# Two graph layers on one core: id transfers tied to a one-column copy, and one gathered bucket of seven in place of two

## The chip, the cores and the metric

The kernel runs on one core of one Trainium2 chip. The metric is the device time of one execution in microseconds (us), as the median of ten runs. A core has five engines that run their own instruction streams and wait for one another by semaphores: TensorE (PE, whose weight loads are shown apart as PEld), VectorE (DVE), ScalarE (ACT), GpSimd (POOL) and SyncE (SP). Plain transfers are issued here mostly from SP's queue; indirect transfers, which fetch rows by a list of row numbers, are issued from POOL's.

## What is computed

A graph has 6,250 nodes with 128 channels each and 200,000 edges (src, dst), sorted by dst. Two attention layers follow one another, each with a residual and a layer norm:

```python
# layer 0
hij = concat([h[src], h[dst]], -1)
exp_e = exp(leaky_relu(hij @ w, 0.2) @ a)
att = exp_e / segment_sum(exp_e, src)[src]
x = layernorm(x + segment_sum(h[src] * att, dst))

# layer 1: 4 heads of 32 channels
H = (x @ W) by head
s = exp(leaky_relu(Hs[src] + Ht[dst], 0.2) - max)
alpha = s / (segment_sum(s, src)[src] + 1e-8)
agg = segment_sum(alpha * H[dst], src) + x @ residual_projection
x = layernorm(x + elu(agg))
```

## The kernel before

Nodes are cut into 49 blocks of 128 (`NB`). An edge belongs to a bucket (i, j): i is the block of its source, j that of its destination. Each bucket has 128 slots, one edge per partition at most; `cols` holds, for each slot of each bucket, the row within the block of the edge's two ends, and -1 where the slot is empty. Seven buckets that follow one another are a chunk (`CH = 7`), so a row of 49 buckets has seven chunks. The instruction order on each engine is the order in which the program writes them.

**First stage (`score_edges`).** It loads the edges' ids, sorts them into slots, writes the table of slots to DRAM (`rows_jm`, `rows_im`) and computes the edge scores of layer 0. The ids of block j lie in a window of the sorted list; `find_windows` (L576) estimates where, and writes the row numbers of all windows into the tile `window_row`, one column for each block. `load_ids` (L599) then fetches the src and the dst ids of the next block with two indirect transfers on POOL, whose row numbers are column j of `window_row`. The tiles `ids0` and `ids1` hold a group of up to seven blocks and there are two of each, so a group's transfers wait until `split_ids` (L620) on DVE has read the group before last. `load_ids` is called at eleven fixed places of the prologue (`LOAD`, one block each) and later once for each row j, after its fourth chunk (L927). `split_ids` runs when the first block of a group is begun, three rows ahead of its scores. Nothing but the buffers and `window_row` holds the POOL queue back, so POOL issues whatever transfers have a tile free, far ahead of the place in the program. The work of this stage in `score_chunk` (L817) is six bf16 matmuls for each bucket on PE (L834), one operation for each bucket on DVE (L844), a one-hot over two rows of slots on DVE (L813), and transposes (L850).

**Layer 0's sum (from L1238).** For each destination block j, bucket by bucket, the weighted rows of the source nodes are needed, one per slot. There are two ways to get them. By PE: a one-hot of the slots (`OneHots`, L1123: SP fetches a row of slots spread to all partitions, DVE compares it, L1002) is multiplied with a table of the block split into three bf16 parts (`y3`), which takes three matmuls (`gather_b`, L1289); ACT copies the result out of PSUM (L1298). By DMA: an indirect transfer on POOL fetches 128 rows from the table `y_d` in DRAM (`Gathers`, L1073, the transfer at L1106). The constant `GP` says how many buckets of the seven are fetched by DMA, always the last ones of a chunk, and for rows r > 0 only (`by_dma`, L1069):

```python
    CUT = 3
    GP = 2
    BY_PE = CH - GP

    def by_dma(r, c):
        return r > 0 and c % CH >= BY_PE
```

A chunk is worked on in a group of three buckets and one of four (`groups_of_chunk`). For each bucket DVE also makes a weighted one-hot of the destinations (L1304), and one f32 matmul (two passes, two records in the trace) adds the bucket to the block's sum in PSUM (L1320). `scatter_loop` (L1049) puts the sums two groups behind the gathers. After each group, generators in `running` take one step: among them `nodes` (L1176), which runs once for each seven finished blocks and holds the layer norm, the products with layer 1's weights and the writing of `h_d` and `res_d` by SP (L1200, L1201). SP's queue also carries the fetches of the slots (L1142), in program order.

**Layer 1's sum (from L1337).** The same by source block i, with the table `h_d`, 132 columns wide (four heads of 32 channels and a one): `gather_c` (three bf16 matmuls for a bucket, L1419), `weigh_c` (a product with the attention weights on DVE, L1436, one operation for the buckets from PSUM and one for those gathered; a one-hot, L1443) and `sum_c` (L1457, f32, two records each). Between them stand the scores of the next row (L1367, L1368), whose one-hots of the sources are made by ACT (L997, L998) for all seven buckets. The one-hots of the destinations are made for all seven buckets too here, as the scores need them.

`Gathers.get` keeps five chunks of gathered rows ahead of their use, out of seven buffers. `Gathers.__init__` computes the row numbers of all gathered buckets on DVE (L1089), `GP` operations for each layer.

Of the kernel before, what the change touches and what calls it, by code (L numbers as in the profile page):

```python
# [11 lines left out]
I32 = mybir.dt.int32  # L12
# [4 lines left out]
P = 128  # L17
# [465 lines left out]
def score_edges(tc, keep, x, src, dst, w0, a0, rows_jm, rows_im):  # L483
# [4 lines left out]
    nc = tc.nc  # L488
# [26 lines left out]
    with ExitStack() as pools:  # L515
# [4 lines left out]
        fa = pools.enter_context(tc.tile_pool(name="fa", bufs=2))  # L520
# [41 lines left out]
        window_row = fc.tile([P, NB], I32, name="window_row")  # L562
# [36 lines left out]
        def load_ids():  # L599

            j = len(loaded_ids)
            if j == NB:
                return
            b = next(b for b, (c0, c1) in enumerate(id_groups) if c0 <= j < c1)
            c0, c1 = id_groups[b]
            if j == c0:
                ids[b] = [fi.tile([P, CH, WT], I32, name=f"ids{k}") for k in range(2)]
            for to, flat in zip(ids[b], (src, dst)):
                if j == NB - 1:
                    nc.sync.dma_start(to[:, j - c0, :], flat[E - WT * P :].rearrange("(p t) -> p t", t=WT))  # L610
                    continue
                nc.gpsimd.indirect_dma_start(  # L612
                    out=to[:, j - c0, :],
                    out_offset=None,
                    in_=flat[: NR * WT].rearrange("(r t) -> r t", t=WT),
                    in_offset=bass.IndirectOffsetOnAxis(ap=window_row[:, j : j + 1], axis=0),
                )
            loaded_ids.append(j)

# [244 lines left out]
        with tc.tile_pool(name="n0", bufs=3) as n0:  # L864
# [22 lines left out]
            for b in range(NB):  # L887
                if b % CH == 0 and b // CH + 2 < NC:
                    load_x(b // CH + 2)

                tp = pa[0].tile([P, 512], F32, name="u")[:, :P]
                nc.tensor.transpose(tp, xcs[b // CH][:, b % CH, :], ident)
                xt = n0.tile([P, P], F32, name="xt")
                nc.scalar.activation(xt, tp, AF.Copy)
                turned.append((b, xt))
                if b > 0:
                    tables(*turned.pop(0))
                if b == LOAD[0]:
                    find_windows(sampled)
                if b in LOAD:  # L900
                    load_ids()
                if b in BEGIN:
                    finding.append(find_slots(BEGIN.index(b)))
                    begun += 1
                if b >= BEGIN[0]:
                    find_more()
                if b == FIRST:
                    for k in range(3):
                        fetch(k)
                    one_hot(0)  # L910
                    one_hot(1)
                if b > FIRST and b % 4 == 0 and CH * (scored + 1) < b and scored + 1 < NC:
                    score_chunk(scored)
                    scored += 1
# [3 lines left out]
        for k in range(scored, len(order)):  # L918
            j, c = order[k]
            if c == 0 and j > 0:  # L920
                if j + AHEAD < NB:
                    finding.append(find_slots(j + AHEAD))
                elif j + 1 == NB:
                    finding.append(check_slots())
            score_chunk(k)
            find_more()
            if c == 3:  # L927
                load_ids()
# [6 lines left out]
def bucketed(ctx, tc, x, w1, al, ar, wr, out, cols, ex, den, rows_jm, rows_im):  # L935
    nc = tc.nc
# [122 lines left out]


    CUT = 3
    GP = 2
    BY_PE = CH - GP
    assert NB % CH == 0

# [7 lines left out]
    class Gathers:  # L1073


        def __init__(self, pool, table, which, ahead, width):
            self.pool, self.table, self.ahead, self.width = pool, table, ahead, width
            base_i = consts.tile([P, NC, GP], I32, name=f"base_i{which}")
            nc.gpsimd.iota(base_i, pattern=[[CH * P, NC], [P, GP]], base=BY_PE * P, channel_multiplier=0)
            base = consts.tile([P, NC, GP], F32, name=f"base{which}")  # L1080
            nc.vector.tensor_copy(base, base_i)

            self.ids = consts.tile([P, NB, NC, GP], I32, name=f"ids{which}")
            for q in range(GP):
                if which == 0:
# [536 lines left out]
@with_exitstack  # L1622
def kernel(ctx, tc, x, src, dst, w0, a0, w1, al, ar, wr, out):
    nc = tc.nc
    ctx.enter_context(tc.manual_schedule())
    NB = -(-x.shape[0] // P)
    keep = ctx.enter_context(tc.tile_pool(name="keep", bufs=1))
    dram = ctx.enter_context(tc.tile_pool(name="slots_d", bufs=1, space=bass.MemoryType.DRAM))
    rows_jm = dram.tile([NB, 2, NB, P], BF16, name="rows_jm")
    rows_im = dram.tile([NB, 2, NB, P], BF16, name="rows_im")  # L1630
    cols, ok, ex, den = score_edges(tc, keep, x, src, dst, w0, a0, rows_jm, rows_im)
    fits = nc.values_load(
        ok, min_val=0, max_val=1, skip_runtime_bounds_check_because="a product of two comparisons is 0 or 1"
    )
    with tc.If(fits == 1) as cmp:
        bucketed(tc, x, w1, al, ar, wr, out, cols, ex, den, rows_jm, rows_im)
    with cmp.Else():
        any_edges(tc, x, src, dst, w0, a0, w1, al, ar, wr, out)
# [35 lines left out]
```

## Time and profile before

| what | value |
|---|---|
| median of ten runs | 3640.07 us (3636.04 to 3643.8) |
| the profiled execution, its own time | 3636.17 us |
| its span, from the first to the last instruction | 3634.3 us |
| mean granted TensorE clock | 0.970 |
| PE busy | 3365.6 us (93% of the span) |
| DVE busy | 3177.8 us (87%) |
| ACT busy | 2027.2 us (56%) |
| POOL busy | 1496.1 us (41%) |
| indirect transfers of rows, layer 0 (`y_d`) | 672, mean 990 ns on POOL |
| indirect transfers of rows, layer 1 (`h_d`) | 672, mean 1065 ns on POOL |
| indirect transfers of ids | 96, mean 1122 ns (src) and 993 ns (dst) on POOL |

The profile is that of one execution. A row of it names an engine, a line of the code, the tiles it writes and reads, the number of instructions and the mean length of one. Lengths of instructions of one engine overlap where they are pipelined, so a group's busy time can be much less than number times mean; on PE that is the rule. The chain of waits follows the work that ended last back from the end, at each step to what released it; pieces of it on one engine add up without overlap, so they are the right place to read what one more instruction costs on that engine. The stages are, by their windows in the trace: prologue to about 90 us, first stage to 1518 us, layer 0's sum from about 1565 to 2510 us, layer 1's sum from about 2535 to 3560 us, and an end of some 70 us.

### The profile page before, as it was taken

Reading aid. Unit: us, or ns where it says so; the run is one execution under the profiler, and the core shown is the slowest. Engines: PE = TensorE matmul, PEld = TensorE weight load, DVE = VectorE, ACT = ScalarE, POOL = GpSimd, SP = SyncE. Lnnn points to the kernel's source line nnn. Section 1 sums busy time; section 2 is a strip of 40 time slices with the busy share of each in tenths; the row PEclk is TensorE's granted clock in tenths of the full one; section 3 lists DMA queues with packets and bytes.
Section 4 is the critical chain, followed back from the end, with each engine's and each line's share of the span. In section 5 each row is a group of like instructions: output and inputs, shape, how many; then the busy total and the mean of one; then the engine's idle time right before and its main releaser. Section 6 shows DMA issues by size and latency. Waiting matters only on the chain.

```text
span 3634.3 us, 125212 instructions
## 1 busy us (share of the span) xinstructions
PE 3365.6 (93%) x50166; PEld 3226.5 (89%) x50166; DVE 3177.8 (87%) x11723; ACT 2027.2 (56%) x3036; POOL 1496.1 (41%) x1474
## 2 busy tenths in 40 slices
PE   4699999999999999799999999997999999999996
PEld 3589989898989899788988988987999999999996
DVE  5688888888888888698888888888999999999997
ACT  4556666666666666343333333334666666666665
POOL 4001010101000000157766766764577676777771
PEclk7899999999999999899999999998999999999998
DMA  2133333343334433444444444445666676666662
GB/s 62 38 126 118 117 118 120 117 124 116 121 115 121 116 120 122 145 124 115 116 113 115 116 113 114 116 114 145 189 202 190 201 201 196 197 200 203 189 197 82
DMA packets 348224, 496.41 MB, mean 137 GB/s; under 512 B 65806, under 2 KB 325347, under 8 KB 347634
## 3 DMA queue, kind: packets, MB, share of 16 engines
q1 hardware_dynamic: 296520, 393.32, 36.0%
q0 software_dynamic: 46992, 94.52, 11.3%
q8 instruction: 399, 6.54, 0.7%
q14 instruction: 191, 1.56, 0.2%
q10 hardware_dynamic: 4122, 0.47, 0.1%
HBM read 472.71 MB, written 15.39 MB: 134 GB/s over the span
## 4 chain that ended last, share of the span: by engine, by line
PE 73%; DVE 16%; ACT 5%; issue 3%; DMA 3%; another core or an unknown queue 0%; POOL 0%; SPq 0%; ACTq 0%; DVEq 0%; POOLq 0%
PE u L1457 16%; PE oj L1320 14%; PE u L834 14%; PE he L1419 8%; PE ye L1289 7%; DVE junk L844 3%; PE tp L850 2%; PE sm L736 2%; DMA rows<-rows_jm 2%; DVE rows L813 2%; PE u L684 2%; PE sp L1368 2%; PE sm L673 1%; PE u L682 1%; DVE vst L711 1%
## 5 line engine op out<-in xcount | busy, mean ns | idle before, releaser
L834 PE MATMUL u<-pq,rows 128*128 128x130 bf16 x14406 | 914.9, 221 | 62.5 <-DVE junk L844 57.0
L834 PEld LDWEIGHTS <-rows 128*128 128x128 bf16 x14406 | 857.2, 98 | 76.3 <-issue 67.0
L1106 POOL DMA_INDIRECT rows_g<-h_d,ids x672 | 716.0, 1065 | 343.6 <-DVE z L1436 175.1
L1106 POOL DMA_INDIRECT rows_g<-y_d,ids x672 | 665.2, 990 | 293.7 <-PE oj L1320 151.3
L1304 DVE TENSOR_SCALAR oh<-iota_b,dsts,ex 128x128 f32<-128x128 bf16 x2401 | 668.8, 361 | 72.5 <-ACT dsts L1282 48.3
L1457 PE MATMUL u<-z,oh 128*128 128x132 f32 x4802 | 700.6, 286 | 0.0
L844 DVE SCALAR_TENSOR_TENSOR junk<-u,a_ext 128x130 bf16<-128x130 f32 x2401 | 547.6, 292 | 89.6 <-PE u L834 87.8
L1457 PEld LDWEIGHTS u<-z,oh 128*128 128x128 f32 x4802 | 592.1, 190 | 0.8
L852 ACT ACTIVATE oh<-tp 128x896 bf16<-128x896 bf16 x343 | 314.4, 917 | 451.5 <-PE tp L850 451.5
L1298 ACT ACTIVATE yc<-ye 128x384 f32<-128x384 f32 (+2 forms) x686 | 298.2, 438 | 478.1 <-PE ye L1289 462.3
L1320 PE MATMUL oj<-yc,oh 128*128 128x128 f32 x3458 | 542.5, 289 | 13.4 <-ACT yc L1298 11.0
L1320 PEld LDWEIGHTS oj<-yc,oh 128*128 128x128 f32 x3458 | 445.7, 194 | 17.1 <-ACT yc L1298 12.7
L1289 PE MATMUL ye<-y,rows 128*128 128x128 bf16 x5187 | 409.5, 222 | 51.7 <-DVE rows L1002 50.8
L1443 DVE TENSOR_TENSOR oh<-iota_b,cols 128x384 f32<-128x384 bf16 (+2 forms) x693 | 421.0, 608 | 0.0
L1419 PE MATMUL he<-h,rows 128*128 128x132 bf16 x5187 | 416.8, 221 | 0.0
L1289 PEld LDWEIGHTS <-rows 128*128 128x128 bf16 x5187 | 354.7, 100 | 69.7 <-DVE rows L1002 32.8
L612 POOL DMA_INDIRECT ids<-in_src_dram,window_row x48 | 53.9, 1122 | 763.8 <-DVE tmp L632 730.6
L1419 PEld LDWEIGHTS <-rows 128*128 128x128 bf16 x5187 | 358.2, 97 | 10.2
L1436 DVE TENSOR_TENSOR z<-he,w 128x396 f32<-128x396 f32 (+2 forms) x693 | 339.3, 490 | 24.5 <-PE he L1419 23.3
L997 ACT ACTIVATE rows<-rows,minus_p 128x896 bf16<-128x896 bf16 x336 | 346.2, 1030 | 23.4 <-DMA rows<-rows_im 13.2
L998 ACT ACTIVATE rows<-rows 128x896 bf16<-128x896 bf16 x336 | 319.3, 950 | 10.6
L1002 DVE TENSOR_SCALAR rows<-rows,part_f 128x896 bf16<-128x896 bf16 (+1 forms) x693 | 286.3, 414 | 6.6 <-DMA rows<-rows_im 3.2
(209 smaller groups left out, 4655.8 us busy)
## 6 DMA issues: line engine op xcount, KB each, us to landing
rows<-rows_jm SPq DMA_DIRECT2D x693, 224.0 KB
rows<-rows_im SPq DMA_DIRECT2D x686, 224.0 KB
rows<-rows_jm SPq DMA_DIRECT2D x336, 160.0 KB
rows_g<-y_d,ids POOLq DMA_INDIRECT x672
rows_g<-h_d,ids POOLq DMA_INDIRECT x672
h_d<-hx SPq DMA_DIRECT2D x6, 462.0 KB
xc<-in_x_dram SPq DMA_DIRECT2D x6, 448.0 KB
x_sb<-in_x_dram POOLq DMA_DIRECT2D x6, 448.0 KB
```

The costliest lines, as they stand in the source:

```text
L834: nc.tensor.matmul(u[:, d, :], rows[:, w, i - c0, :], pq3[:, b, w, s, :], start=(w == 0 and s == 0), stop=(w == 1 and s == 2),)
L844: nc.vector.scalar_tensor_tensor(junk, u[:, d, :], 0.0, a_ext, op0=OP.max, op1=OP.mult, accum_out=acc[:, i : i + 1])
L997: nc.scalar.activation(rows, rows, AF.Square, bias=minus_p)
L998: nc.scalar.activation(rows, rows, AF.Relu, bias=1.0, scale=-1.0)
L1106: nc.gpsimd.indirect_dma_start(out=t[:, q, :], out_offset=None, in_=self.table[:, :], in_offset=bass.IndirectOffsetOnAxis(ap=self.ids[:, r ...
L1289: nc.tensor.matmul(ye[:, k, :], oh[:, i0 + k - c0, :], y3[:, i0 + k, s, :], start=(s == 0), stop=(s == 2))
L1304: nc.vector.tensor_scalar(oh[:, k, :], iota_b, dsts[0][:, i : i + 1], ex[:, j, i : i + 1], op0=OP.is_equal, op1=OP.mult,)
L1320: nc.tensor.matmul(outs[j], oh[:, k, :], values[k], start=(i == 0), stop=(i == NB - 1))
L1419: nc.tensor.matmul(he[:, k, :], oh[:, j0 + k - c0, :], h3[:, j0 + k, s].rearrange("p h e -> p (h e)"), start=(s == 0), stop=(s == 2),)
L1436: nc.vector.tensor_tensor(z[:, a:b].rearrange("p n (h e) -> p n h e", h=H), rows.rearrange("p n (h e) -> p n h e", h=H), weights[i][:, j0 ...
L1443: nc.vector.tensor_tensor(oh[:, :n], iota_b[:, None, :].to_broadcast([P, n, P]), cols[:, j0 : j0 + n, 0, i : i + 1].to_broadcast([P, n, P] ...
L1457: nc.tensor.matmul(aggs[i], oh[:, k, :], z[:, k, :], start=(j == 0), stop=(j == NB - 1))
```

## The change

`load_ids` first copies column j of `window_row` into a small tile `row` of its own, on DVE, and the two transfers take their row numbers from that tile. The tile comes from the pool `fa`, which has two buffers for each name, so a copy also waits until the transfers of two blocks before have read theirs. For the last block, whose ids come by two plain transfers on SP, the copy is made but not used. And `GP` is 1 in place of 2, so `BY_PE` is 6: of each chunk of seven buckets, six come by PE and one by an indirect transfer, in both layers. The number of row numbers, the tiles of gathered rows (`[P, GP, width]`), the slots fetched for layer 0's one-hots (`needed`) and the parts of `weigh_b` and `weigh_c` follow from `GP`.

```diff
@@ load_ids
                 ids[b] = [fi.tile([P, CH, WT], I32, name=f"ids{k}") for k in range(2)]
+
+            row = fa.tile([P, 1], I32, name="row")
+            nc.vector.tensor_copy(row, window_row[:, j : j + 1])
             for to, flat in zip(ids[b], (src, dst)):
...
-                    in_offset=bass.IndirectOffsetOnAxis(ap=window_row[:, j : j + 1], axis=0),
+                    in_offset=bass.IndirectOffsetOnAxis(ap=row, axis=0),
@@ bucketed
     CUT = 3
-    GP = 2
+    GP = 1
     BY_PE = CH - GP
```

## The prediction

> **What bounds the kernel now.** I read the chain of waits first, by engine, and then the busy time of each engine by stage.
>
> ```profile
> PE 73%; DVE 16%; ACT 5%; issue 3%; DMA 3%; another core or an unknown queue 0%; POOL 0%; SPq 0%; ACTq 0%; DVEq 0%; POOLq 0%
> ```
>
> POOL, whose work the change halves, has no share of the chain. The stages (columns: window, length, busy us of PE, PEld, DVE, ACT, POOL with their instructions, granted clock, DMA share, GB/s):
>
> ```profile
> 90.00:1510.00 1420.00, 1327.60 (x24436) 1253.58 (x24435) 1208.05 (x5930) 885.00 (x1078) 58.84 (x54) 0.97 0.37 115
> 1600.00:2450.00 850.00, 807.38 (x9003) 788.33 (x9000) 740.09 (x2578) 319.14 (x819) 607.83 (x620) 0.99 0.47 115
> 2560.00:3580.00 1020.00, 1018.41 (x14501) 995.81 (x14500) 988.98 (x2438) 655.86 (x750) 702.00 (x658) 1.00 0.67 193
> ```
>
> Layer 0's sum (second line) leaves PE idle 42.6 us of 850, layer 1's (third) 1.6 of 1020. A busy PE could still hide waits, so I checked it against the chain, whose pieces do not overlap. One whole chunk of layer 0:
>
> ```profile
> 1917.65 0.50 PE ye L1289 x9
> 1918.15 0.72 PE oj L1320 x6
> 1918.87 0.34 PE ye L1289 x6
> 1919.21 0.95 PE oj L1320 x8
> ```
>
> These are nothing but matmuls end to end, 2.51 us: nine and six bf16 gathers (three buckets and two), and the sums of seven buckets. In row 0, where no bucket is gathered by DMA, the second group has four buckets by PE:
>
> ```profile
> 1571.56 0.67 PE ye L1289 x12
> 1572.23 0.95 PE oj L1320 x8
> ```
>
> 0.67 us for 12 against 0.34 for 6: each bf16 matmul takes 0.056 us of the chain, with gathers by DMA or without. In layer 1 the matching pieces are:
>
> ```profile
> 3003.04 0.35 PE he L1419 x6
> 3003.39 0.95 PE u L1457 x8
> 3004.35 0.52 PE he L1419 x9
> ```
>
> That is 0.058 us for each matmul (132 columns).
>
> **Part 1, GP from 2 to 1: what it adds on PE.** In each layer rows 1 to 48 have 7 chunks, so 336 buckets move to PE, three matmuls each: 1008 for a layer, with as many weight loads, which overlap (98% of PE's stretch in layer 1 shows PEld busy beside it). Layer 0: 1008 x 0.0556 (0.50 / 9) = 56.0 us. Layer 1: 1008 x 0.0584 (mean of 0.35 / 6 and 0.52 / 9, rounded up) = 58.9 us. PE sets the end in both, so both lie on the path: 114.9 us.
>
> **What it takes away.** 672 indirect transfers, about 1.03 us of POOL each, some 690 us of POOL. The waits of both windows say who waits for whom:
>
> ```profile
> POOL rows_g L1106 <- PE oj L1320: 114.0, 211, 5.5
> POOL rows_g L1106 <- DVE z L1436: 175.1, 225, 16.4
> ```
>
> POOL waits for the users of its buffers; of its 1344 gathers no engine but POOL itself is recorded as waiting for one (0.9 us). The gain is therefore nothing. If the five chunks that it fetches ahead were not cover enough, this could be worth something; the third rival prices that.
>
> **What moves on the other engines.** ACT copies 384 columns in place of 256 in layer 0 (490 against 382 ns): 336 x 0.108 = 36 us on an engine busy 319 of 850, one group ahead of its use; nothing. DVE's one-hot there covers 768 slots; the rows on each side are 381 ns (640) and 446 ns (896), so +0 to +65 ns, by position +32 ns, 11 us over the layer on an engine with 110 us free; nothing in the steady chunk. In layer 1 the weighing is 561 + 284 ns where it was 420 + 418: +7 ns a chunk, 2 us. DVE is 97% busy there, but PE's chunk grows by 0.175 us from 2.98, so DVE's share falls; without that cover it would cost 2 us. SP fetches 192 KB in place of 160 for a chunk of layer 0, while POOL's two gathers of 64 KB become one: 256 KB in place of 288. L1089 runs once in place of twice for each layer (753 ns): in layer 0's start it is in the chain, -1 us.
>
> **What gives some of it back.** Layer 0 stops PE after every seventh row, where `nodes` puts its steps on DVE and its two writes ahead of the next slots on SP's queue (the rows of slots issued behind them land after 6.7 us). Over the layer:
>
> ```profile
> PE ye L1289 <- DVE rows L1002: 24.3, 12, 2.7
> ```
>
> Two such stops per seven rows, 1.2 to 1.4 and 2.73 us, and one of 2.7 us at the layer norm (PE busy 7.34 of 10 us from 1825). They begin when PE has used up the two chunks of one-hots made ahead. Each chunk now lasts 0.167 us longer, so each stop shrinks by about 0.33 us: 3 x 0.33 x 6 = 6 us. The bounds: none (the larger rows land later by as much) to 20 us, as a shorter stop may keep the clock up too. After the 2.73 us stop the granted clock falls:
>
> ```profile
> 1717.00:1721.00 4.00, 1.27 (x13) 1.09 (x12) 2.53 (x9) 1.99 (x5) 1.94 (x2) 0.78 0.19 58
> 1721.00:1726.00 5.00, 5.00 (x34) 4.88 (x33) 5.00 (x18) 0.88 (x2) 0.17 (x1) 0.50 0.20 44
> ```
>
> Five us at half rate cost 2.5 us, up to 15 us over six stops. I take 6, from the stops alone: 2.4 us is nearer to 2.73, which lost the clock, than to 1.4, which did not. In layer 1 I take 1 us back, of PE's 1.6 us idle.
>
> [...]
>
> **Part 2, the copy.** 49 copies of one column on DVE. No row shows this one; the nearest are 141 ns for an operation on one column (L1408) and 191 ns for a copy of 98 columns (L746). So 49 x 0.1 to 0.19, 5 to 9 us of DVE, and 37 of the 49 lie in the first stage's rows. There the copy follows the fourth chunk, just ahead of the one-hot L813; in the row from 528 us that place is followed by DVE waiting 0.40 and 0.31 us for PE's L834, and the chain there is on PE. The copy is hidden by that wait; without it 37 x 0.14 = 5 us. Queued behind it on DVE stand L813 and the L844 that PE's PSUM buffers wait for. The copy waits for transfers issued two rows (55 us) before: no wait. POOL now issues two transfers per row and not 14 in a burst. Seven rows with a burst take 198.3 us (x24 pieces of L834 at 273.57, 471.87, 670.24), without one 197.8 (1066.00 to 1263.82); in a burst the splits L632 stretch from 0.28 to 0.49 us. Four bursts in the loop: -2 to -3 us. In the prologue POOL ran from 21.8 to 77 us without a pause; now the last ids of the second group are issued one block (about 3 us) ahead of the split that reads them. Two gathers at 1.25 us and a landing of at most 2.25 us (last issue 24.18, first split 26.43) make 4.75 us, so 0 to 2 us of wait for DVE. For the part: between -3 and +9 us, taken as -2 + 0 + 0.
>
> [...]
>
> **Sum.** 56.0 - 6 + 58.9 - 1 - 1 - 2 = 104.9 us on top of the profiled 3636.17 us: 3741. That execution lies 3.9 us under the median of 3640.07, so for a median the forecast is 3745 us. Its own range: -14 (half of the clock's 15 us too, and 6 in the first stage) to +11 (copies uncovered, stops unchanged): 3731 to 3756.
>
> **Rivals.** (a) *The stops in layer 0 mostly vanish.* For: they arise from DVE work and a late transfer, both measured against PE's pace, and each drags the clock. Against: 0.33 us of cover against stops of 1.4 and 2.7. Price: 42.6 us idle and 15 of clock; two thirds gone are 38 us in place of 6: 3713. (b) *Pacing turns into a wait.* For: in the prologue DVE has in-order work behind a copy that waits for two transfers to land. Against: the 2.25 us landing. Price: three waits of 2 us, 37 copies at 0.19 uncovered, no burst gain: 6 + 7 + 2 = 15: 3760. (c) *The gathers set PE's pace and its records only hide it*, so that halving them pays. For: two gathers take 2 x (0.94 + 0.30) = 2.5 us of POOL, almost the chunk's 2.51. Against: the same 0.056 us a matmul in row 0 without gathers, and POOL's waits. It decides if PE's own work in a chunk is under 2.51 - 0.17 = 2.34 us; at 2.2 us the layers would lose 0.14 x 672 = 94 us: 3546; at the point itself no change. (d) *The copy paces nothing*, as POOL would be as late anyway: -2 becomes 0, 3747, within the forecast.
>
> **How the numbers follow.** Forecast with (d) 0.78, (a) 0.09, (b) 0.11, (c) 0.02. The time is the forecast's, 3745. The range 3724 to 3760 takes in the half of (a) nearest to it and most of (b). A measurement tells 0.2% (7 us) from no change; only (c) is not slower by that: faster 0.02, same 0.01, slower 0.97.
>
> **What would show it.** Right: the chunk's chain in layer 0 reads 0.50, 0.72, 0.50, 0.95; layer 0's and layer 1's sums each last 50 to 59 us longer; 672 row gathers in all; seven rows of the first stage at 197.8 us or less throughout. Wrong: L1289 at other than 5187 + 1008 = 6195 matmuls, a DVE wait at the copy, or PE idle in layer 0 well under 35 us or over 45.

## The result, and the profile after

| | before | after |
|---|---|---|
| median | 3639.78 us (28 runs) | 3740.50 us (8 runs, 3737.01 to 3741.57) |
| profiled execution, its span | 3636.17, 3634.3 us | 3741.09, 3739.3 us |
| mean granted clock | 0.970 | 0.974 |

The ratio is 1.0274 with a 95% interval of [1.0265, 1.0283]: slower by 2.7%, or 100.7 us between the medians (96.5 to 103.0 by the interval). The forecast was 3745 us.

Where the 105.0 us between the two spans lie can be read from the first and the last matmul of each stage (us):

| | to the first score | first stage | gap | layer 0 | gap | layer 1 | end |
|---|---|---|---|---|---|---|---|
| before | 87.0 | 1429.5 | 25.3 | 969.1 | 23.5 | 1042.2 | 57.7 |
| after | 89.2 | 1430.4 | 25.0 | 1015.4 | 24.3 | 1094.8 | 60.2 |
| difference | +2.2 | +0.9 | -0.3 | +46.3 | +0.8 | +52.6 | +2.5 |

So the two layers' sums took nearly all of it. The shares of the chain of waits after:

```profile
PE 75%; DVE 15%; ACT 5%; issue 3%; DMA 2%; another core or an unknown queue 0%; POOL 0%; SPq 0%; ACTq 0%; POOLq 0%; DVEq 0%
```

PE's share rose by two points and POOL still has none. Windows of layer 0 and layer 1 as before (window, length, busy us of PE, PEld, DVE, ACT, POOL with their instructions, granted clock, DMA share, GB/s):

```profile
1600.00:2450.00 850.00, 814.08 (x9421) 796.33 (x9421) 706.41 (x2442) 338.01 (x785) 284.07 (x297) 0.99 0.36 98
2590.00:3610.00 1020.00, 1019.80 (x14852) 1004.50 (x14851) 963.22 (x2335) 638.85 (x729) 359.70 (x313) 1.00 0.55 167
```

POOL's busy time in the layers has halved (607.83 to 284.07 us, 702.00 to 359.70), and no time was won by it; in layer 0 PE's idle time in this window fell from 42.6 to 35.9 us. The groups of the two gathers by PE:

```profile
L1422 PE MATMUL he<-h,rows 128*128 128x132 bf16 x6195 | 476.0, 221 | 0.0
L1292 PE MATMUL ye<-y,rows 128*128 128x128 bf16 x6195 | 465.0, 221 | 46.6 <-DVE rows L1005 45.7 <-DVE y L1260 0.9
```

Each has 5187 + 1008 = 6195 matmuls. Two groups of layer 0 that follow one another, in the chain of waits (start, us, what; ... stands for 0.43 us of products of `nodes`):

```profile
2001.77 0.50 PE ye L1292 x9
2002.28 0.95 PE oj L1323 x8
...
2003.66 0.50 PE ye L1292 x9
2004.16 0.72 PE oj L1323 x6
```

Both gathers of a chunk now have nine matmuls at 0.50 us; the sums beside them are as long as before (0.95 and 0.72 us). POOL's own waits show the pacing:

```profile
POOL ids L615 <- DVE row L610: 1080.0, 45, 29.1
```

POOL now waits 45 times for the copy, 1080 us in all, where before the change it issued up to fourteen transfers in a row in the first stage's rows and 44 in the prologue (21.8 to 77.0 us).

### The profile page after: what moved, and what is told of

Read it like the earlier page. It is cut to its first block, busy times and chain, and to the rows that moved or that the text cites. A ratio compares the mean times of both kernels' runs of the same rounds, so it can differ in the third digit from the quotient of the medians.

```text
span 3739.3 us, 128005 instructions
## 1 busy us (share of the span) xinstructions
PE 3478.9 (93%) x52182; PEld 3345.5 (89%) x52182; DVE 3201.5 (86%) x11770; ACT 2062.8 (55%) x3036; POOL 825.5 (22%) x802
## 4 chain that ended last, share of the span: by engine, by line
PE 75%; DVE 15%; ACT 5%; issue 3%; DMA 2%; another core or an unknown queue 0%; POOL 0%; SPq 0%; ACTq 0%; POOLq 0%; DVEq 0%
PE u L1460 16%; PE u L837 14%; PE oj L1323 14%; PE he L1422 10%; PE ye L1292 8%; DVE junk L847 3%; PE tp L853 2%; PE sm L739 2%; PE u L687 2%; DVE rows L816 2%; PE sp L1371 2%; DVE vst L714 2%; PE sm L676 1%; PE u L685 1%; PE sp L1370 1%
## 5 line engine op out<-in xcount | busy, mean ns | idle before, releaser
L837 PEld LDWEIGHTS <-rows 128*128 128x128 bf16 x14406 | 857.3, 98 | 74.9 <-issue 65.5
L1307 DVE TENSOR_SCALAR oh<-iota_b,dsts,ex 128x128 f32<-128x128 bf16 x2401 | 671.3, 353 | 111.0 <-PE oj L1323 86.6
L1323 PE MATMUL oj<-yc,oh 128*128 128x128 f32 x4130 | 619.4, 287 | 10.7 <-ACT yc L1301 9.4
L1301 ACT ACTIVATE yc<-ye 128x384 f32<-128x384 f32 (+1 forms) x686 | 334.1, 490 | 496.7 <-PE ye L1292 489.6
L1109 POOL DMA_INDIRECT rows_g<-h_d,ids x336 | 384.8, 1145 | 725.5 <-DVE z L1439 687.9
L1323 PEld LDWEIGHTS oj<-yc,oh 128*128 128x128 f32 x4130 | 523.1, 194 | 13.5 <-ACT yc L1301 11.2
L1292 PE MATMUL ye<-y,rows 128*128 128x128 bf16 x6195 | 465.0, 221 | 46.6 <-DVE rows L1005 45.7
L1109 POOL DMA_INDIRECT rows_g<-y_d,ids x336 | 326.7, 972 | 676.8 <-PE oj L1323 599.1
L1422 PE MATMUL he<-h,rows 128*128 128x132 bf16 x6195 | 476.0, 221 | 0.0
L1292 PEld LDWEIGHTS <-rows 128*128 128x128 bf16 x6195 | 410.2, 99 | 64.2 <-DVE rows L1005 27.8
L1439 DVE TENSOR_TENSOR z<-he,w 128x396 f32<-128x396 f32 (+1 forms) x693 | 389.6, 562 | 55.7 <-PE he L1422 39.3
L1422 PEld LDWEIGHTS <-rows 128*128 128x128 bf16 x6195 | 417.3, 97 | 10.2
L1005 DVE TENSOR_SCALAR rows<-rows,part_f 128x896 bf16<-128x896 bf16 (+1 forms) x693 | 297.8, 431 | 5.4 <-DMA rows<-rows_im 5.0
L615 POOL DMA_INDIRECT ids<-in_src_dram,row x48 | 55.1, 1148 | 1102.6 <-DVE row L610 1080.0
```

The lines of the kernel that those rows point to most:

```text
L837: nc.tensor.matmul(u[:, d, :], rows[:, w, i - c0, :], pq3[:, b, w, s, :], start=(w == 0 and s == 0), stop=(w == 1 and s == 2),)
L1109: nc.gpsimd.indirect_dma_start(out=t[:, q, :], out_offset=None, in_=self.table[:, :], in_offset=bass.IndirectOffsetOnAxis(ap=self.ids[:, r ...
L1292: nc.tensor.matmul(ye[:, k, :], oh[:, i0 + k - c0, :], y3[:, i0 + k, s, :], start=(s == 0), stop=(s == 2))
L1301: nc.scalar.activation(yc[:, :m], ye[:, :m], AF.Copy)
L1307: nc.vector.tensor_scalar(oh[:, k, :], iota_b, dsts[0][:, i : i + 1], ex[:, j, i : i + 1], op0=OP.is_equal, op1=OP.mult,)
L1323: nc.tensor.matmul(outs[j], oh[:, k, :], values[k], start=(i == 0), stop=(i == NB - 1))
```

## The experiments

Runs that were made together share one chip, with the kernel before beside them. The first four came to lie on a chip where the kernel before takes 4147.86 us (median of 23 runs) in place of 3640. The other eight lay on three chips where it takes 3639 to 3644. A ratio is to the kernel before on the same chip.

**1. Two gathers to one, without the copy (e1_gp1_only).**

```diff
-    GP = 2
+    GP = 1
```

> One bucket of seven gathered by DMA in both layers, no copy in the ids' loading. Theory (nearly all of the change is the 2016 matmuls added to PE, of which some 15 us come back in waits that the stages already held; the copy is worth 3 us at most): 97 to 101 us over the kernel before, within 4 us of the changed kernel. Rival (the copy and the pacing cost or save 10 us and more, hidden in the sum): over 10 us away from the changed kernel, on either side.

**2. The copy and its pacing, without the gathers (e2_copy_only).**

```diff
+            row = fa.tile([P, 1], I32, name="row")
+            nc.vector.tensor_copy(row, window_row[:, j : j + 1])
...
-                    in_offset=bass.IndirectOffsetOnAxis(ap=window_row[:, j : j + 1], axis=0),
+                    in_offset=bass.IndirectOffsetOnAxis(ap=row, axis=0),
```

> The copy and the transfers tied to it alone, two buckets gathered as before. Theory, from the stages of the two traces (prologue +2.2 us, first stage +0.9 us): 0 to +4 us over the kernel before. Prediction's term: -2 us. Rival (pacing turns into a wait): +10 to +15 us.

**3. The copy is made, but the transfers do not use it (e3_copy_unused).** Only the first two lines of that diff.

> The copy is made on DVE, but the transfers take their row numbers from the old tile, so POOL is not paced. Theory (49 copies of 0.15 us are hidden in DVE's waits): within 2 us of the kernel before. Rival (the copies' own time is what the first stage loses): +3 us or more, as much as with the pacing.

**4. Less for DVE in layer 1 (e4_light_dve).** Three of the four one-hots of the second group are left out, and those of an earlier chunk used in their place, so a part of layer 1's sum is wrong.

```diff
+            skip = 3 if j0 % CH == CUT and n == CH - CUT else 0
             nc.vector.tensor_tensor(
-                oh[:, :n],
+                oh[:, skip:n],
```

> The kernel before with less DVE work in layer 1's sum: of the one-hots for a chunk's second group only one in place of four is computed, the other three are taken from the first group (left out: those three one-hots, 0.40 us of DVE a chunk). Theory (in the kernel before DVE holds 29 us of the chain in layer 1's sum although PE reads as 99.8% busy, because short waits hide inside the modelled lengths of matmuls): 10 to 25 us faster than the kernel before, all in layer 1. Rival (PE's recorded idle time of 1.6 us is all there is to win): at most 3 us faster.

Measured on the chip of 4147.86 us (stages from the profiled executions, us):

| run | median | ratio | to the first score | first stage | layer 0 | layer 1 |
|---|---|---|---|---|---|---|
| e1_gp1_only | 3831.32 | 0.9236 [0.922, 0.9253] | 120.3 | 1474.7 | 1020.5 | 1096.8 |
| e2_copy_only | 4060.81 | 0.9784 [0.9765, 0.9803] | 86.6 | 1430.0 | 1139.5 | 1293.7 |
| e3_copy_unused | 4150.28 | 1.0005 [0.9994, 1.0015] | 120.5 | 1476.7 | 1140.2 | 1295.9 |
| e4_light_dve | 4163.29 | 1.0031 [1.0018, 1.0045] | 120.5 | 1484.7 | 1132.3 | 1314.9 |

None of the expectations had this in it: here each part of the change makes the kernel faster, in its own stages. Pacing gives 34 us before the first score and 47 in the first stage; one gather in place of two gives 120 us in layer 0 and 199 in layer 1. With its part made, each stage is as long as on the other chips (after: 89.2, 1430.4, 1015.4, 1094.8). What differs is visible in the chain of waits of e3_copy_unused, which has no part of the change that acts:

```profile
PE 68%; DVE 17%; issue 8%; ACT 5%; DMA 1%; another core or an unknown queue 1%; POOL 0%; SPq 0%; ACTq 0%; DVEq 0%; POOLq 0%
```

"issue", time in which an engine waited for nothing that the profile shows, has 8% in place of 3. In the waits from 20 to 120 us of the same run, where POOL issues transfers of ids every 1.25 us (line waited for, us in total, times, longest):

```profile
PEld L686 <- issue: 21.6, 15, 10.0
PE u L686 <- issue: 19.5, 8, 10.0
DVE pqr L478 <- issue: 15.0, 1, 15.0
```

PE and DVE stood still up to 10 and 15 us at a time there; with the pacing the longest such stand in the same stretch is 2.7 us (PEld L675 in e2_copy_only), as long as in the kernel before on its own chip (PEld L673, 2.7). A window of layer 1 with two gathers for a chunk (e2_copy_only):

```profile
2700.00:3700.00 1000.00, 867.39 (x11464) 808.04 (x11465) 797.89 (x1925) 542.50 (x610) 544.49 (x521) 0.99 0.54 159
```

and with one (e1_gp1_only):

```profile
2700.00:3700.00 1000.00, 1000.00 (x14553) 985.28 (x14553) 944.86 (x2285) 627.61 (x716) 361.52 (x314) 1.00 0.55 167
```

With two, PE is idle 133 us of 1000, and no engine is full (DVE 798 us); with one PE is idle for none. So less work for DVE had little to lift there, and e4_light_dve, whose theory expected a gain, is no test of it: it was repeated below. That it came out 7 to 19 us slower is not explained by these runs.

**5. The changed kernel once more (r5_after), and 6. with a second gather whose rows nobody reads (r6_idle_gathers).** These and the next two on a chip where the kernel before takes 3641.88 us.

```diff
+                idle = self.pool.tile([P, GP, self.width], F32, name="idle_g")
+                nc.gpsimd.indirect_dma_start(
+                    out=idle[:, 0, :],
...
```

> The changed kernel itself, again. Theory A (the stops of the first runs come only where indirect transfers follow each other closely, and the changed kernel has none that do): its stages are the same on either kind of chip, sum of layer 0 near 1015 us and of layer 1 near 1095, time 3735 to 3755 us; so 2.7% slower where the kernel before takes 3640 us, and 9 to 10% faster where it takes 4148. Rival B (that chip is slower in itself, and the two parts of the change each mend something of their own there): the two parts' gains, 316 and 87 us, need not add up; a time over 3790 us where the kernel before takes 4148.

> The changed kernel with one more gather for each chunk in both layers, whose rows nobody reads: POOL issues two transfers for each chunk again as before the change, while PE's work stays that of the changed kernel. Theory A (transfers that follow each other closely stop the other engines on some chips): where the kernel before takes 4148 us, layer 0 goes back from 1020 to about 1140 us and layer 1 from 1097 to about 1295, 3745 to 4060; where it takes 3640 us, the time stays at 3741 (to 3750), since no engine waits for POOL. Rival (c) of the prediction (the gathers set PE's pace, its records only hide it): the time follows the number of gathers on every chip, so more than 30 us slower than the changed kernel where the kernel before takes 3640.

r5_after took 3738.77 us (1.0269 [1.0252, 1.0286]) and r6_idle_gathers 3744.57 (1.0284 [1.0267, 1.0302]). Layer 0 and layer 1 with the idle gathers:

```profile
1600.00:2450.00 850.00, 810.78 (x9353) 793.00 (x9351) 711.37 (x2423) 336.58 (x781) 570.55 (x587) 0.99 0.48 120
2590.00:3610.00 1020.00, 1020.00 (x14857) 1004.92 (x14855) 964.27 (x2336) 640.92 (x729) 693.58 (x630) 1.00 0.67 188
```

POOL is as busy as before the change, and PE goes on as in the changed kernel: 672 more gathers cost 5.8 us, not the 30 and more of rival (c). So on this chip the number of gathers did not set the time. This run was not made on the chip of 4147.86 us, nor was the changed kernel itself. By the stages of e1_gp1_only and e2_copy_only the changed kernel would take some 3746 us there (86.6 + 1430.0 + 24.6 + 1020.5 + 23.6 + 1096.8 + 61.8, and 2 around the span); this is an estimate.

**7. The moved bucket with one matmul in place of three (r7_one_matmul).** Two of its three bf16 parts are left out of the result in both layers.

```diff
-                    for s in range(3):
+                    parts = 1 if j > 0 and (i0 + k) % CH == BY_PE - 1 else 3
+                    for s in range(parts):
```

> The changed kernel, with the bucket that was moved from a gather to PE multiplied by one of its three parts only; the other two parts (the lower bits) are left out of its result in both layers. 672 matmuls fewer in each layer, nothing else changed. The prediction's price (0.0556 us for each matmul in layer 0, 0.0584 in layer 1, PE sets the end): 37 + 39 us less, less some 4 us for longer stops, 3741 to 3669, up to 3680. Rival (in layer 1 DVE held part of the chain, which PE's busy time hides): layer 0 33 to 37 us shorter, layer 1 only 28 to 34. Second rival (the cost sits in the group of four buckets and its copies, not in the matmuls): under 30 us less in all.

**8. No gathers at all (r8_no_gathers).** `GP = 0`.

> The changed kernel with the last gathered bucket moved to PE as well, in both layers: 1008 more matmuls in each layer, no indirect transfers there. By the price that the change itself measured (46 us in layer 0, 53 in layer 1): 3741 + 99 = 3840 us; by the prediction's full price with all stops left as they are: 56 + 59, 3856. If the gather that is left still costs PE something on a chip where the kernel before takes 4148 us, less than 3830 there.

r7_one_matmul took 3670.39 us (1.008 [1.0063, 1.0097]), 68.4 us less than r5_after: 27.6 in layer 0, 39.5 in layer 1. The expectation gave 33 and 39 to the matmuls, so the cost is mostly in them (why layer 0 has less is shown in the next section); the rival for layer 1 (28 to 34) fell, for these 672. r8_no_gathers took 3864.67 us (1.0616 [1.0598, 1.0634]), 126 more than r5_after and not 99 to 115: 48.7 in layer 0, as expected, but 82.4 in layer 1. There the code has groups of three, three and one for each chunk when no bucket is gathered, and the sums in the chain read (... stands for the gathers between them):

```profile
3107.06 0.33 PE u L1460 x2
...
3107.56 0.73 PE u L1460 x6
...
3108.81 0.73 PE u L1460 x6
```

The seven sums take 0.73 + 0.73 + 0.33 = 1.79 us, where groups of three and four take 0.73 + 0.95 = 1.68: 0.11 us for each of the 336 chunks whose grouping changed, or 37 us by these pieces, where 82.4 - 58.9 leaves 23.5 to explain. Layer 1 of this run measures another grouping too, and is a poor test of the price.

**9. The copy alone, again (r9_copy_only), and 10. less for DVE in layer 1, again (r10_light_dve).** The edits of 2 and 4, on a chip where the kernel before takes 3643.54 us.

> The kernel before with the copy and its pacing alone, two gathers for each chunk kept; again, for a chip where the kernel before takes about 3640 us. The prediction: -2 us, bounds -3 to +9: 3638 (3637 to 3649), first stage and prologue within 3 us of the kernel before. Rival (b), pacing becomes a wait: 3650 to 3655, prologue 6 us longer. Rival (d), the copy paces nothing: 3640, and transfers still in bursts in POOL's timeline. Where the kernel before takes 4148 us: 4061 once more.

> The kernel before, with three of the four one-hots of the second group of buckets left out in layer 1 (older ones are used in their place, so part of layer 1's sum is wrong); PE's work is unchanged and DVE has some 0.4 us less in each chunk of 2.98 us. Again, for a chip where the kernel before takes about 3640 us. Theory (DVE held PE in layer 1 before the change, hidden in PE's busy time, so the moved matmuls cost 52.6 us and not 58.9): layer 1 gets 6 to 25 us shorter, time 3615 to 3634. Rival (PE is full there, as its busy time says): layer 1 within 2 us of the kernel before, 3638 to 3642; the price per matmul was then too high. Where the kernel before takes 4148 us: 4163 once more, which tells nothing of this.

r9_copy_only: 3642.29 us, 0.9996 [0.9988, 1.0005], which is -1.3 us (-4.4 to +1.8); first stage 1427.8 us, prologue 87.4. Rival (b) of the prediction fell; whether the copy gains 2 us or nothing is below what these runs tell. On the undisturbed chips the first stage lasted 1426.0 to 1430.4 us in the eight profiles with the copy and 1429.5 in the two without. r10_light_dve: 3632.81 us, 0.9974 [0.9965, 0.9984], 6 to 13 us less. Layer 1 before and with the lighter DVE:

```profile
2560.00:3570.00 1010.00, 1008.93 (x14407) 986.57 (x14406) 980.53 (x2422) 655.07 (x748) 702.00 (x658) 1.00 0.68 195
```

```profile
2560.00:3570.00 1010.00, 1008.62 (x14474) 992.37 (x14472) 894.30 (x2433) 658.27 (x751) 667.69 (x658) 1.00 0.67 195
```

PE reads 1008.6 to 1008.9 us busy in both, and yet does 67 matmuls more in the same stretch with the lighter DVE: the modelled ends of the matmuls had covered its waits. Layer 1 lasted 1037.6 us, where three profiles with all of DVE's work and two gathers have 1042.2, 1042.0 (r9_copy_only) and 1044.1 (r11_copy_spread). The gain of 4.4 to 6.5 us is at the low end of what the theory expected or under it, and outside the rival's 2 us. Where it lies is shown in the next section.

**11. nodes' steps at every third group of layer 0 (r11_copy_spread, with the copy and two gathers), and 12. the same in the changed kernel (r12_after_spread).** The same result is computed. In the changed kernel PE still stopped after every seventh row. In the chain of waits of after, such a place (... stands for pieces left out):

```profile
1718.33 0.96 PE oj L1323 x8
...
1719.60 1.07 DVE ha L1209
1720.67 0.33 DVE rows L1005
1721.00 0.77 DVE oh L1307 x3
1721.77 0.99 DVE hst L1216
...
1727.91 1.01 DVE hx L1223
1728.92 0.02 issue
1728.95 0.96 ACT h L1224
...
1731.20 0.68 PE ye L1292 x9
```

Here the chain leaves PE for 12 us, in which PE first uses up what lies ready and then stands idle three times, for 0.55, 0.21 and 2.75 us: between the one-hots that PE needs (L1005, L1307) lies at each group a step of `nodes` of about 1 us on DVE (L1209, L1216), and one step holds DVE for longer, as DVE's L1223 is followed by a wait for ACT's L1224. The edit takes one step in three groups, but for the last two of the eight chunks of nodes:

```diff
+    def each_third(steps):
+        for _ in steps:
+            yield
+            yield
+            yield
...
-                        running.append(nodes(*next(c for c in node_chunks if c[1] == j + 1)))
+                        c = next(c for c in node_chunks if c[1] == j + 1)
+                        running.append(each_third(nodes(*c)) if c[1] < NB - 2 else nodes(*c))
```

> The kernel with the copy and its pacing, two gathers for each chunk, and in layer 0 the steps of nodes taken at every third group in place of every group (but for the last two of its eight chunks of nodes). What it computes is the same. Theory (the stops in layer 0 are DVE's: a step of about 1 us of nodes at each group on top of the one-hots): most of the 4.5 us of stops per seven rows go, and the clock they cost: layer 0 15 to 40 us shorter, time 3603 to 3628 where the kernel before takes 3641. Rival (the stop of 2.7 us comes from the row of slots that lands late behind nodes' two writes on SP's queue): that stop and its clock stay, layer 0 only 6 to 12 us shorter, 3631 to 3637. Where the kernel before takes 4148 us: PE is stopped there by something else, 4035 to 4061.

> The changed kernel with the same spreading of nodes' steps. Theory: its stops per seven rows (0.65, 0.20, 2.75 us and the clock) go too, and with them goes what the longer chunks gave back: layer 0 12 to 35 us shorter than 1016, time 3705 to 3728; the change itself (this run against the other of this call) then costs 52 to 55 us in layer 0 and not 46 to 48. Rival: stops stay, 3730 to 3740. Where the kernel before takes 4148 us: 3705 to 3730 also, as no two gathers follow each other closely (theory A of the runs before), or over 3760 if that chip's loss is of another kind.

On a chip where the kernel before takes 3639.21 us: r11_copy_spread 3614.53 us, 0.9926 [0.9913, 0.9939]; r12_after_spread 3703.38 us, 1.0173 [1.016, 1.0186]. Layer 0 lasted 938.8 and 981.6 us. The window in layer 0 of r11_copy_spread:

```profile
1600.00:2450.00 850.00, 829.68 (x9310) 811.40 (x9308) 764.25 (x2667) 333.72 (x856) 643.82 (x644) 0.99 0.48 119
```

PE's idle time is 20.3 us where it was 42.6, and layer 0 is 30.9 us shorter than in r9_copy_only: in the range of the theory, and far over the 6 to 12 us of the rival (a row of slots that lands late). But of the 4.5 us of stops per seven rows that the theory named, only about half went. The stop of 1.42 us went, that of 0.37 shrank to 0.17, and with them went one of 1.71 us at the layer norm, which the theory had not counted; the stop of 2.73 us stayed, at 2.2 to 2.3 us. It belongs to one step of `nodes` (L1223 with ACT's L1224 above, L1228 and L1229 in this run), which spreading does not divide. Before the stop that ends at 2019 us:

```profile
2016.17 1.01 DVE hx L1228
...
2017.21 0.95 ACT h L1229
```

The rival had a small part in the stop of 1.42 us: in the kernel before, the chain goes through a row of slots there, for which DVE waited 0.36 us at 1988 us. r11_copy_spread beats both kernels, the one beside it by 25 us and the changed one (3740.50 us) by 126. r12_after_spread came out 2 us under its range (3705 to 3728). There that step stops PE for 1.7 to 1.8 us in place of 2.75. The second half of r12's expectation failed: the change costs 42.8 us in layer 0 between these two, not 52 to 55, and the next section says why.

## Why the prediction was right, step by step

**Layer 0, 56.0 - 6.** The direction was right and the size nearly so: +46.3 us, where the sum had 56 - 6 and took 1 off for L1089. The prediction's own sign of being right, 50 to 59 us in layer 0, was missed. The account can be closed. Beside the stage's length, two sums over windows of 1 us within layer 0 were taken: the time PE was idle, and the time lost to the clock (one minus the granted clock). Then for four pairs, the last three each of one chip:

| from, to | matmuls x 0.0556 | PE idle | lost to the clock | sum | measured |
|---|---|---|---|---|---|
| before, after | +56.0 | 55.9 to 47.9 | 18.7 to 17.0 | +46.3 | +46.3 |
| r7_one_matmul, r5_after | +37.4 | 53.9 to 48.1 | 25.4 to 18.9 | +25.1 | +27.6 |
| r5_after, r8_no_gathers | +56.0 | 48.1 to 41.7 | 18.9 to 18.9 | +49.6 | +48.7 |
| r11, r12 (spread) | +56.0 | 30.7 to 24.5 | 15.6 to 10.1 | +44.3 | +42.8 |

From before to r7_one_matmul the same rows give +23.4 against +20.1, so the account closes to about 3 us. L1089 has no place in it: it runs before the first matmul of the layer (at 1533.7 us, the layer begins at 1541.8), and the gap ahead of the layer shrank by 0.3 us, not 1.

So 0.0556 us for a matmul held, and 6 us of shorter stops were forecast where 5.8 to 8.0 were measured. The manner was not as told, with 0.33 us off each of three stops. For seven rows PE has five stops. Two are around the layer norm, of 0.95 and 1.71 us, which the prediction read as one of 2.7; they became 0.76 and 1.66. The two that wait for DVE's one-hots shrank from 1.42 and 0.37 us to 0.55 to 0.74 and 0.21. The one of 2.73 us stayed (2.75): it is one step of `nodes` in which DVE subtracts for 1.0 us, waits for ACT (L1221 in the kernel before, 0.96 us) and then does small parts, before it comes to the next one-hot. A longer chunk of PE's work did not hide it, and run 11 shows that spreading the steps does not either. The clock did not come back with the stops in the first pair, as the sum had assumed; in the others it gave 0 to 6.5 us, inside the half of 15 us that the range had taken in, and it is why the 42.8 of the last pair and the 27.6 of the second are low.

Where the clock was lost stands beside the stops. After the one of 2.75 us that ends at 1731 us, with stops of 0.55 and 0.21 us in the 7 us before it, the granted clock in the changed kernel reads:

```profile
1731.00:1734.00 3.00, 2.79 (x26) 2.74 (x27) 3.00 (x10) 1.04 (x3) 0.00 (x0) 0.73 0.00 0
1734.00:1737.00 3.00, 3.00 (x28) 2.93 (x27) 3.00 (x12) 0.76 (x2) 0.94 (x1) 0.71 0.21 70
```

0.73 and 0.71 over three us each. In the traces, read in windows of 0.1 us, a stretch at a granted clock of 0.50 stands at each of the six stops of 2.7 us that layer 0 has from 1600 us on in the kernels before and after; it was 3.4 us long at eleven of these twelve and 6.8 at the one that ends at 1720.6 us in the kernel before. By windows of 1 us such a stretch stands at four of the six stops of 2.2 to 2.3 us in r11_copy_spread, and at none of the six of 1.7 to 1.8 us in r12_after_spread. Nor does one stand at the stops of 0.2 to 1.8 us between 1600 and 2450 us in the kernels before and after, so rival (a)'s "each drags the clock" held for one stop in five.

**Layer 1, 58.9 - 1.** Measured +52.6: this is the step that failed, "in layer 1 I take 1 us back, of PE's 1.6 us idle". 6.3 us came back, and PE's busy time was no bound for it. The traces show where. Once in each row PE transposes the row maximum that DVE has just made. One such place before:

```profile
2999.75 0.36 DVE L1396 TENSOR_REDUCE m<-score 128x1 f32<-128x196 f32 x1
3000.16 0.27 PE L1401 MATMUL u<-ident,m 128*1 128x128 f32 x1
```

and after:

```profile
3006.06 0.36 DVE L1399 TENSOR_REDUCE m<-score 128x1 f32<-128x196 f32 x1
3006.67 0.27 PE L1404 MATMUL u<-ident,m 128*1 128x128 f32 x1
```

Before, the transpose starts 0.05 us after the maximum is ready, and so in most rows: PE had waited for it. After, the maximum is ready 0.25 us ahead. From the start of the matmul before it to the start of the transpose pass 0.18 us in the middle row before the change and 0.06 after. The matmul before it is recorded as 0.22 us long, so a wait of 0.12 us lies inside it and PE reads busy. The sum of these steps over 48 rows (the first row's lies ahead of the layer's first matmul), taken off the length of layer 1 (us):

| run | layer 1 | steps to the transpose | the rest |
|---|---|---|---|
| before | 1042.2 | 9.9 | 1032.3 |
| r9_copy_only | 1042.0 | 9.3 | 1032.7 |
| r11_copy_spread | 1044.1 | 11.2 | 1032.9 |
| r10_light_dve | 1037.6 | 4.5 | 1033.1 |
| r7_one_matmul | 1054.9 | 3.3 | 1051.6 |
| after | 1094.8 | 3.1 | 1091.7 |
| r5_after | 1094.4 | 2.8 | 1091.6 |
| r6_idle_gathers | 1094.6 | 2.7 | 1091.9 |
| r12_after_spread | 1094.6 | 2.9 | 1091.7 |

The rest agrees within 0.8 us among the four runs with two gathers, and within 0.3 among the last four. Between the two groups lie 59 us, or 0.0585 for each of 1008 matmuls, which is the price of the sum. What came back is the wait for DVE's row maximum, once in a row. r7_one_matmul has used it up already with its first 336 matmuls, which is why they cost only 1054.9 - 1042.2 = 12.7 us, 0.038 each, and the other 672 (to r5_after) 39.5, 0.0588 each. And r10_light_dve, which takes DVE's work away with PE's unchanged, wins its 4.6 us in the same place. The prediction had the row in hand, DVE busy 989 of 1020 us, and used it only for what it would cost to cover 2 us. The chain's share of DVE in layer 1 is no measure of it: 28.9 us in before and 14.8 in r9_copy_only, two executions with layer 1 equally long.

**Gathers removed, 0.** Right here: r6_idle_gathers put them back and PE kept its pace. There, where the kernel before takes 3641.88 us, 672 more gathers cost 5.8 us. On the chip of the first four runs the same gathers cost 120 and 199 us. So that "no engine but POOL itself is recorded as waiting" settles it for the chip that was profiled, and nothing in that profile tells of the other.

**The copy, -2.** Within the error: -1.3 us (-4.4 to +1.8) by r9_copy_only, and no wait at the copy. The first stage had 1427.8 us with it and 1429.5 without. The copy takes 154 ns on DVE, 7.5 us for all 49, and e3_copy_unused shows no cost of it alone (1.0005 [0.9994, 1.0015], at most 6 us).

**Left out of the sum.** The end, from the last matmul of layer 1 on, lasts 60.1 to 60.2 us in the five profiles of a changed kernel with its gather (after, 5, 6, 7 and 12) and 57.3 to 59.3 in four with two gathers: some 2 us, whose cause was not looked into. The 2.2 us before the first score are within the scatter of the profiled runs (86.3 to 89.2 with the copy). So the sum of 104.9 against 105.0 is partly luck: it was 5.3 us too high in layer 1 and 2.7 in layer 0, and 8.1 too low in the rest (-2 forecast, +6.1 measured: 2.2 before the first stage and 0.9 in it, 0.5 in the gaps, 2.5 at the end). It also compares two single executions; between the medians the change cost 100.7 us, 4 less than the sum.

**Rivals.** (a) fell: PE's idle time in layer 0 shrank by 8 of 56 us. (b) and (c) fell by runs 9 and 6. (d) is half answered: the copy does pace POOL (45 waits, two transfers at a time), but whether that is worth 2 us or nothing these runs can't tell.

## What to carry to other kernels

Price work that is moved to the bound engine by the duration in the chain of waits, and take back what the engine's waits leave. A busy share of 99.8% does not mean that there are none: look for the places, once a row here, where the bound engine starts right after another engine's result, as a short wait can lie inside the recorded length of the matmul before it (0.12 of 0.22 us here). More work ahead of such a place hid the wait here (the steps to the transpose took 9.9 us before and 3.1 after), and so did less work on the other engine (4.5 in r10_light_dve). Steps of a side job that are put between the bound engine's inputs stop it by their bunching and not by their sum: one in three groups in place of one in each gave 31 us of 970 with the same work (9 and 11). The step that goes to another engine and back was not helped much by this (2.73 to 2.2 us). Work off the critical path may be free only on the chip on which it was seen, as the gathers were (5.8 us on one chip, 120 and 199 on another): measure a kernel with many indirect transfers on more than one.

## What the runs showed of the hardware

The kernel before takes 3639 to 3644 us wherever else it ran and 4147.86 on one chip. All runs on that chip were made together, so these runs can't tell the chip from its condition at that hour. The granted clock in e3_copy_unused's profile is 0.951 against 0.970, which makes (1 - 0.951) x 4139.8 - (1 - 0.970) x 3634.3 = 94 us at most of the 508, an estimate from these four numbers. In e3_copy_unused, where POOL issues indirect transfers one after another (two for each chunk, or a burst every 1.25 us), PE, DVE and ACT stop without a wait that the profile shows, for up to 10.0 us (L686), 15.0 (L478) and 7.0 (L662) at a time. Such idle times of PE and its weight loads sum to 100.4 us at the scores' matmuls (L836) and to 90.0 at layer 1's sums (L1459), where the kernel before on its own chip has 67.0 (L834) and none (L1457). POOL's own durations are the same in both: 0.95 and 0.94 us for one, 0.30 between two. With at most two transfers for a row of the first stage (e2_copy_only) they sum to 67.0 us at L836 from 30 to 1500 us, and with one for a chunk of the layers (e1_gp1_only) PE is idle for none of the 1000 us from 2700. What the engines wait for was not shown. A PE that stands idle for 10 us with nothing to wait for, as above, is the sign to look for.
